# A GRU scan on one core: both rows of x on ScalarE's DMA queue, and r's first products two chunks at a time

## The chip, the cores and the metric

The kernel runs on one core of a Trainium2 chip. The metric is device time in microseconds of one execution, median over runs; lower is better. A profiled execution gives a span as well, from the first to the last instruction of the program, which is a little shorter than the time. Engines are named as in the profile: PE (TensorE), with PEld for its weight loads, DVE (VectorE), ACT (ScalarE), POOL (GpSimd) and SP (SyncE); ACTq, SPq and POOLq are the DMA-issuing sides of those engines.

## The reference

A GRU runs over 128 steps of x (64 batch rows, 128 steps, 512 features), and its states are added to x. After every fourth step but the last the state goes through one more layer.

```python
def step(h, inp):
    x_t, prop = inp
    comb = jnp.concatenate([x_t, h], axis=-1)
    z = jax.nn.sigmoid(comb @ Wz + bz)
    r = jax.nn.sigmoid(comb @ Wr + br)
    comb2 = jnp.concatenate([x_t, r * h], axis=-1)
    h_cand = jnp.tanh(comb2 @ Wh + bh)
    h_new = (1.0 - z) * h + z * h_cand
    h_next = jnp.where(prop, jnp.tanh(h_new @ Wp + bp), h_new)
    return (h_next, h_new)
_, ys = jax.lax.scan(step, h0, (xs, do_prop))
# returned: x + transpose(ys)
```

Wz, Wr and Wh are 1024 x 512; their upper half multiplies x, their lower half h (or r * h). Everything is float32.

## The kernel before

**Tiling.** The batch of 64 is split into two halves of 32 rows (S = 2, V = 32), and the 512 output features into four blocks of 128. A product is written as several matmuls of 128 x 32 weights against 256 columns, each of which fills a block of 32 partitions of a PSUM bank; four of them stand side by side. K = 4 counts the chunks of 128 features over which a product is summed. In the trace each float32 matmul shows as two records.

**Products with x.** The parts of the gates that depend on x alone are made ahead of the recurrence. For step 0 and step 1 they are plain products: `plain(t, (i,))` gives for gate i (0 is r, 1 is z, 2 is the candidate) four units, one for each chunk k, and `now` runs units for both halves at once. Later steps take them in groups of four steps with a Strassen-like scheme (`batch`, `batches`), whose operands POOL and DVE sum up. They fill the gaps between the recurrent products (`fill`).

**Order.** The schedule is manual: the instructions of each engine run in the order in which the program emits them. An engine that waits holds all that stands behind it on that engine.

**The start**, around which the change lies:

- Lines 137 to 141: two rows of x, steps 0 and 1, each 64 x 512 float32 (128 KB), go into `x_rows`, step 0's over SP's queue and step 1's over ACT's (`both_queues`).
- Lines 142 and 143: `load_wx(R, k0, k1)` loads the upper half of Wr in three pieces over SP's queue: chunk 0 (256 KB), chunk 1 (256 KB), and chunks 2 and 3 (512 KB). z's and the candidate's upper halves follow in two pieces each (line 151), then step 2 of x in four (`load_step`, line 122), and further on the lower halves, `wh`.
- Line 145: the biases come over POOL's queue. Line 147: a sigmoid on one element makes ACT load its table early.
- Line 154: a copy of one element of `wx` on POOL waits for r's third piece; behind it POOL issues the loads of h0 (line 156).
- `idle(n)` (line 236) runs n matmuls on zeros (128 x 32 against 512 columns of bf16). `idle(28)` is the first thing on PE.
- `turn_rows(0, ...)` and `turn_rows(1, ...)` (line 306) transpose the rows of step 0 and step 1 on PE, four transposes each, and DVE copies the result into `xT` (line 311). All eight transposes stand on PE ahead of r's first product.
- `split_bias` (lines 205 to 210) is work of DVE. Then come four more fillers, and r's products: chunk 0 of step 0, chunk 0 of step 1, chunk 1 of step 0, chunk 1 of step 1, and then chunks 2 and 3 of the one and of the other. Step 0's go to bank `scratch_q`, step 1's to `scratch_a`; line 246 is the matmul of all products.
- Then follow z's first chunks (`scratch_r`, `scratch_x`), the biases spread over the partitions (line 217), z's other chunks, the candidate's (`scratch_y`), the first eight units of step 2, and the recurrence (`half`).

SP's DMAs each signal one of eight semaphores in rotation; from the ninth DMA on, an issue waits for the landing of the one eight places before it.

Of the kernel before, what the change touches and what calls it, by code (L numbers as in the profile page):

```python
# [18 lines left out]
def kernel(  # L19
# [14 lines left out]
    nc = tc.nc  # L34
    B, T, D = x.shape
# [7 lines left out]
    K = D // P  # L43
# [52 lines left out]
    def part(q):  # L96
        return slice(q * V, (q + 1) * V)
# [15 lines left out]
    both_queues = (nc.sync, nc.scalar)  # L113
# [12 lines left out]
    def load_wx(i, k0, k1):  # L126
# [10 lines left out]
    x_rows = one.tile([P, Q4, S, J], F32, tag="xs0", name="x_rows")[:B].rearrange(  # L137
        "b t h u -> b (t h u)"
    )
    for t in range(2):  # L140
        both_queues[t].dma_start(out=x_rows[:, ts(t, D)], in_=x[:, t, :])  # L141
    for k0, k1 in ((0, 1), (1, 2), (2, K)):
        load_wx(R, k0, k1)
    for i, b in enumerate((br, bh, bz)):
# [10 lines left out]
    for h in range(S):  # L155
        nc.gpsimd.dma_start(
            out=h_rows[:, h, :],
            in_=h0[ts(h, V), :].rearrange("b (q j) -> q b j", q=NQ),
# [44 lines left out]
    def split_bias():  # L203
        high, low = thirds[:NQ], thirds[2 * V : 2 * V + NQ]
        nc.vector.tensor_copy(high, bias_in)
        nc.vector.tensor_sub(rest, bias_in, high)
        nc.vector.tensor_copy(middle, rest)
        nc.vector.tensor_copy(thirds[V : V + NQ], middle)
        nc.vector.tensor_sub(rest, rest, middle)
        nc.vector.tensor_copy(low, rest)  # L210
# [23 lines left out]
    def idle(n):  # L234
        for i in range(n):
            nc.tensor.matmul(
                rec[i // NQ % 3].rearrange("p a d n -> p (a d n)")[part(i % NQ)],
                lhsT=zeros[:, :V],
                rhs=zeros,
                start=True,  # L240
                stop=True,
            )
# [441 lines left out]
    def now(units):  # L684
        put(units)
        both(len(units))
# [3 lines left out]
    turn_rows(0, scratch[4])  # L690
    turn_rows(1, scratch[3])
    split_bias()
    idle(4)
    for part_k in (slice(0, 1), slice(1, 2), slice(2, K)):
        for t in range(2):
            now(first[R][t][part_k])
    load_wh(R)
# [373 lines left out]
```

## Time and profile before

| | us |
|---|---|
| time, median of 3 runs | 1259.13 (1259.06 to 1259.54) |
| time of the profiled execution | 1258.66 |
| its span | 1256.6 |

The mean granted clock of TensorE was 1.000 over the span.

How to read the lines that follow in the prediction. A row of a timeline has the start and the length in us of a group of equal instructions, engine, line, operation, what it writes and reads, shapes and count, and in brackets the idle time of the engine before it and what released it. A row of stretches has the stretch, its length, then for PE, PEld, DVE, ACT and POOL the busy time with the number of instructions, and at last the granted clock of TensorE, the busy share of the 16 DMA engines and the GB/s that they moved. A row of the chain has start, length and place. A row of waits has the waiting engine and line, the releaser, the total in us, the number of waits and the longest. A row of DMA issues has what was moved, the issuing queue, the count, the KB of one, and the median us from issue to landing. Matmuls are pipelined and their ends are modelled, so the spacing of their starts says more than their lengths.

### The profile page before, as it was taken

Reading aid. Unit: us, or ns where it says so; the run is one execution under the profiler, and the core shown is the slowest. Engines: PE = TensorE matmul, PEld = TensorE weight load, DVE = VectorE, ACT = ScalarE, POOL = GpSimd, SP = SyncE. Lnnn points to the kernel's source line nnn. Section 1 sums busy time; section 2 is a strip of 40 time slices with the busy share of each in tenths; the row PEclk is TensorE's granted clock in tenths of the full one; section 3 lists DMA queues with packets and bytes.
Section 4 is the critical chain, followed back from the end, with each engine's and each line's share of the span. In section 5 each row is a group of like instructions: output and inputs, shape, how many; then the busy total and the mean of one; then the engine's idle time right before and its main releaser. Section 6 shows DMA issues by size and latency. Waiting matters only on the chain.

```text
span 1256.6 us, 60732 instructions
## 1 busy us (share of the span) xinstructions
PE 1248.4 (99%) x25952; PEld 1155.6 (92%) x25952; DVE 809.1 (64%) x2183; ACT 836.3 (67%) x2687; POOL 909.7 (72%) x1032
## 2 busy tenths in 40 slices
PE   9999999999999999999999999999999999999998
PEld 5899999999999999999999999999999999999975
DVE  5666666666666666666666666666666666666554
ACT  2566666666666676666666666666676666666665
POOL 4988777777876788767777677787777787677530
PEclk9999999999999999999999999999999999999999
DMA  7311212121122120121111211111211112111011
GB/s 244 96 32 43 52 36 53 39 52 41 32 53 50 40 52 22 51 54 37 53 30 44 52 47 43 41 46 39 53 37 49 40 37 54 45 45 36 13 37 25
DMA packets 112290, 61.09 MB, mean 49 GB/s; under 512 B 12777, under 2 KB 109301, under 8 KB 112021
## 3 DMA queue, kind: packets, MB, share of 16 engines
q1 hardware_dynamic: 111588, 56.90, 17.0%
q8 instruction: 205, 3.36, 1.2%
q14 instruction: 65, 0.52, 0.1%
q0 software_dynamic: 256, 0.14, 0.1%
q10 hardware_dynamic: 176, 0.16, 0.1%
HBM read 40.38 MB, written 16.78 MB: 45 GB/s over the span
## 4 chain that ended last, share of the span: by engine, by line
PE 98%; DMA 1%; issue 1%; SPq 0%; DVE 0%; POOLq 0%; POOL 0%; ACT 0%; ACTq 0%
PE rec L246 45%; PE rec_z L246 16%; PE scratch_r L246 14%; PE scratch_q L246 11%; PE scratch_a L246 5%; PE scratch_y L246 4%; PE scratch_x L246 4%; DMA wx<-in_L_cond_Wr_dram 0%; SPq L886 0%; DMA out_dram<-xr 0%; SPq L127 0%; POOLq L1066 0%; POOL xr L876 0%; DVE z L980 0%; SPq L141 0%
## 5 line engine op out<-in xcount | busy, mean ns | idle before, releaser
L246 PE MATMUL rec<-wh,rhT 128*32 128x256 f32 x4096 | 376.6, 379 | 0.0
L246 PE MATMUL rec<-wh,hT 128*32 128x256 f32 x3072 | 282.9, 379 | 0.0
L246 PE MATMUL rec_z<-wh,hT 128*32 128x256 f32 x3072 | 282.8, 379 | 0.0
L246 PEld LDWEIGHTS rec<-wh,rhT 128*32 128x32 f32 x4096 | 248.5, 110 | 22.3 <-ACT rec L442 1.2
L281 ACT ACTIVATE scratch_r<-rec 64x128 f32<-64x128 f32 x512 | 128.0, 250 | 132.9 <-PE rec L246 65.3
L442 ACT COPY rec<-cp 64x256 f32<-64x256 f32 x512 | 189.9, 371 | 20.2 <-DVE cp L483 0.3
L246 PEld LDWEIGHTS rec<-wh,hT 128*32 128x32 f32 x3072 | 186.7, 110 | 16.2 <-issue 1.9
L246 PEld LDWEIGHTS rec_z<-wh,hT 128*32 128x32 f32 x3072 | 193.3, 110 | 8.1
L281 ACT ACTIVATE rec_z<-rec_z 64x128 f32<-64x128 f32 x488 | 122.0, 250 | 91.1 <-PE rec_z L246 79.2
L281 ACT ACTIVATE c<-rec 64x128 f32<-64x128 f32 x512 | 138.8, 271 | 60.7 <-PE rec L246 48.8
L876 POOL TENSOR_TENSOR xr<-xr,h 128x256 f32<-128x256 f32 x125 | 109.4, 876 | 85.3 <-DVE h L993 83.0
L621 POOL TENSOR_TENSOR cp<-mb,mb 128x768 f32<-128x768 f32 x76 | 139.2, 1831 | 9.3 <-DVE mb L587 5.7
L621 POOL TENSOR_TENSOR mb<-mb,mb 128x768 f32<-128x768 f32 x58 | 106.3, 1833 | 45.5 <-DVE mb L587 45.5
L621 POOL TENSOR_TENSOR cp<-mb 128x768 f32<-128x768 f32 x46 | 84.3, 1832 | 56.9 <-ACT rec_z L442 55.5
L246 PE MATMUL scratch_r<-tw,s 128*32 128x192 f32 x928 | 120.8, 326 | 0.0
L560 ACT COPY cq<-scratch_q 128x384 f32<-128x384 f32 x212 | 102.0, 481 | 19.2 <-PE scratch_q L246 17.7
L577 DVE TENSOR_TENSOR cx<-scratch_r,cx 128x384 f32<-128x384 f32 x106 | 59.1, 557 | 84.1 <-PE scratch_r L246 68.8
L246 PE MATMUL scratch_q<-tt,s 128*32 128x192 f32 x928 | 103.5, 326 | 0.0
L941 DVE SCALAR_TENSOR_TENSOR keep<-rec_z,h 128x256 f32<-128x256 f32 x91 | 38.6, 425 | 94.8 <-ACT rec_z L281 87.4
L583 DVE TENSOR_TENSOR mb<-scratch_q,cx 128x384 f32<-128x384 f32 x106 | 59.1, 558 | 62.4 <-ACT cq L560 62.4
L918 DVE TENSOR_TENSOR rh<-scratch_r,h 128x128 f32<-128x128 f32 x192 | 56.0, 292 | 61.2 <-ACT scratch_r L281 61.2
L246 PE MATMUL rec<-wp,hT 128*32 128x256 f32 x992 | 91.6, 379 | 0.1
(207 smaller groups left out, 3851.0 us busy)
## 6 DMA issues: line engine op xcount, KB each, us to landing
out_dram<-xr SPq DMA_DIRECT2D x249, 64.0 KB, 1.8
xr<-in_x_dram SPq DMA_DIRECT2D x248, 64.0 KB, 2.3
xs<-in_x_dram SPq DMA_DIRECT2D x240, 64.0 KB, 2.1
wx<-in_L_cond_Wz_dram SPq DMA_DIRECT2D x2, 512.0 KB, 7.8
wx<-in_L_cond_Wh_dram SPq DMA_DIRECT2D x2, 512.0 KB, 9.1
wh<-in_L_cond_Wr_dram SPq DMA_DIRECT2D x2, 512.0 KB, 7.7
wh<-in_L_cond_Wz_dram SPq DMA_DIRECT2D x2, 512.0 KB, 5.7
wh<-in_L_cond_Wh_dram SPq DMA_DIRECT2D x2, 512.0 KB, 9.4
```

The source lines that it names most:

```text
L246: nc.tensor.matmul(ps[part(2 * h + c)], lhsT=left, rhs=rhs(c), start=start, stop=True, skip_group_check=True,)
L281: nc.scalar.activation(o, v, func)
L442: nc.scalar.copy(gate_ps(i, h)[rows].rearrange("p d (c n) -> p d c n", c=C), G[t][rows, :, :, i, :].rearrange("p c d n -> p d c n"),)
L560: nc.scalar.copy(c[:, :nm], ps[:, :nm])
L577: nc.vector.tensor_add(T2[what][:, :nm], r_ps[:, :nm], T2[what][:, :nm])
L583: nc.vector.tensor_add(blocks(1, 1), runs(q_ps[:, :nm]), runs(T2[what][:, :nm]))
L621: nc.gpsimd.tensor_add(dst, a, b)
L876: nc.gpsimd.tensor_add(o, o, h_new.rearrange("p h (k e) -> p h e k", k=K))
L918: nc.vector.tensor_mul(rh[:, h, :], r_, h_old[:, h, :])
L941: nc.vector.scalar_tensor_tensor(out=kept[0], in0=kept[1], scalar=1.0, in1=kept[2], op0=ALU.subtract, op1=ALU.mult,)
```

## The change

Both rows of x are issued on ScalarE's queue, step 0's first. SyncE's queue so begins with r's weights, whose three pieces stay as they are. On PE two fillers instead of four stand behind the transposes, and r's products of chunks 0 and 1 run for step 0 and then for step 1, where before the steps alternated chunk by chunk. Chunks 2 and 3 run as before. Nothing else on any engine changes its place.

```diff
     for t in range(2):
-        both_queues[t].dma_start(out=x_rows[:, ts(t, D)], in_=x[:, t, :])
+        nc.scalar.dma_start(out=x_rows[:, ts(t, D)], in_=x[:, t, :])
     for k0, k1 in ((0, 1), (1, 2), (2, K)):
         load_wx(R, k0, k1)
...
     turn_rows(0, scratch[4])
     turn_rows(1, scratch[3])
     split_bias()
-    idle(4)
-    for part_k in (slice(0, 1), slice(1, 2), slice(2, K)):
+    idle(2)
+    for part_k in (slice(0, 2), slice(2, K)):
         for t in range(2):
             now(first[R][t][part_k])
     load_wh(R)
```

## The prediction

> **What bounds the kernel now.** I read the page first, its busy shares and its chain; then a table of three stretches; then, inside the first of them, the chain in order of time.
>
> ```profile
> span 1256.6 us, 60732 instructions
> PE 1248.4 (99%) x25952; PEld 1155.6 (92%) x25952; DVE 809.1 (64%) x2183; ACT 836.3 (67%) x2687; POOL 909.7 (72%) x1032
> PE 98%; DMA 1%; issue 1%; SPq 0%; DVE 0%; POOLq 0%; POOL 0%; ACT 0%; ACTq 0%
> 0.00:14.00 14.00, 11.73 (x176) 6.28 (x180) 7.75 (x22) 2.41 (x5) 3.97 (x12) 1.00 0.81 264
> 14.00:1240.00 1226.00, 1225.93 (x25608) 1141.49 (x25604) 794.54 (x2139) 826.08 (x2655) 904.84 (x1019) 1.00 0.18 46
> ```
>
> In the two rows of stretches the first column after the length is the busy time of PE: from 14 to 1240 us it is busy for 1225.93 of 1226.00 us. Nothing that this change touches lies there, and no instruction of that stretch changes. So the edit can move only the moment at which PE becomes continuous, and everything behind it slides by the same amount. That moment is in the first 14 us, where 14.00 - 11.73 = 2.27 us of PE are idle.
>
> ```profile
> 0.75 0.62 SPq L141
> 1.43 0.80 SPq L127
> 2.27 0.52 SPq L127
> 2.84 6.12 DMA wx<-in_L_cond_Wr_dram
> 9.01 1.07 PE scratch_q L246 x16
> 10.08 0.86 PE scratch_a L246 x16
> 10.94 0.86 PE scratch_r L246 x16
> 11.81 0.86 PE scratch_x L246 x16
> PE rec L236 <- DVE zeros L67: 1.2, 1, 1.2
> PE scratch_q L246 <- DMA wx<-in_L_cond_Wr_dram: 1.1, 1, 1.1
> ```
>
> The chain (start, length, what) says what the start hangs on: SP issues x's row of step 0, then r's three weight loads (256, 256 and 512 KB), and PE goes continuous at 9.01 when the third has landed at 8.96. The waits of PE put 1.1 us on that load. The other idle time is the 1.2 us before the first filler, which stays. Call the three loads c0, c1 and c2.
>
> **The change part by part.** First the queue. Removing the x issue from SP's head takes 1.43 - 0.75 = 0.68 us from in front of c0, c1, c2 and all that SP issues behind them. With the same lengths c0 is issued at 0.75, c1 at 1.59, c2 at 2.12 us.
>
> ```profile
> wx<-in_L_cond_Wr_dram SPq DMA_DIRECT2D x2, 256.0 KB, 4.3
> wx<-in_L_cond_Wr_dram SPq DMA_DIRECT2D x1, 512.0 KB, 6.1
> x_rows<-in_x_dram SPq DMA_DIRECT2D x1, 128.0 KB, 3.3
> x_rows<-in_x_dram ACTq DMA_DIRECT2D x1, 128.0 KB, 2.8
> 2.00:3.00 1.00, 1.00 (x16) 0.43 (x12) 0.22 (x1) 0.85 (x2) 1.00 (x3) 1.00 0.84 242
> 3.00:4.00 1.00, 1.00 (x16) 0.20 (x8) 0.00 (x0) 0.00 (x0) 0.21 (x1) 1.00 0.51 123
> 4.00:5.00 1.00, 1.00 (x10) 0.70 (x6) 0.00 (x0) 0.00 (x0) 0.00 (x0) 1.00 0.82 256
> 5.00:6.00 1.00, 1.00 (x13) 0.57 (x15) 0.85 (x2) 0.00 (x0) 0.00 (x0) 1.00 0.92 309
> 8.00:9.00 1.00, 0.00 (x0) 0.00 (x0) 0.95 (x3) 0.00 (x0) 0.00 (x0) 1.00 1.00 326
> ```
>
> The last number of the issue rows is the time from issue to landing; the last two of the stretches are the busy share of the 16 DMA engines and GB/s. If c2 keeps its 6.1 us, it lands 0.68 us earlier, at 8.28: one bound. The other bound is no shift: the bytes in front of c2's end are the same 2 x 128 + 2 x 256 + 512 KB, and from 5 us on the engines are 0.92 to 1.00 busy, so an earlier issue only helps if the engines have idle time to fill. They have: 0.51 busy from 3 to 4 us and 0.82 from 4 to 5, which is 0.49 + 0.18 = 0.67 us, just while c0 is not flowing yet. I take 0.6 of 0.68, near the upper bound because that hole is as large as the shift; c2 lands near 8.36.
>
> Second, the row of step 1 now goes behind that of step 0 on ScalarE's queue.
>
> ```profile
> 0.76 0.58 ACTq L141 DMA_DIRECT2D x_rows<-in_x_dram  x1
> 1.37 1.28 ACT L147 ACT_TABLE_LOAD   x1 [1.37 <-PEq L1057]
> 12.93 0.65 ACT L226 COPY bias_x<-scratch_y 128x256 f32<-128x256 f32 x2 [10.07 <-PE scratch_y L217]
> 3.73 0.64 PE L236 MATMUL rec<-zeros 128*32 128x512 bf16 x4
> 4.30 0.74 PE L306 MATMUL scratch_y<-ident,x_rows 64*128 64x64 f32 x4
> 4.84 0.68 PE L306 MATMUL scratch_x<-ident,x_rows 64*128 64x64 f32 x4
> 5.45 0.62 PE L236 MATMUL rec<-zeros 128*32 128x512 bf16 x4
> 5.91 0.73 PE L246 MATMUL scratch_q<-wx,xT 128*32 128x256 f32 x8
> 6.45 0.62 PE L246 MATMUL scratch_a<-wx,xT 128*32 128x256 f32 x8
> 6.88 0.62 PE L246 MATMUL scratch_q<-wx,xT 128*32 128x256 f32 x8
> 7.32 0.62 PE L246 MATMUL scratch_a<-wx,xT 128*32 128x256 f32 x8
> 5.56 0.42 DVE L311 COPY xT<-scratch_x 128x256 f32<-128x256 f32 x1
> ```
>
> ScalarE's table load and the dummy sigmoid behind it move by the 0.58 us of an issue; the next work there is at 12.93 after 10.07 us idle, so this costs nothing (without that cover, 0.58). Step 0's row lands at 0.76 + 2.8 = 3.6 us (was 0.75 + 3.3 = 4.05); the fillers run to about 3.73 + 0.43 (their spacing) = 4.16, so its transposes start near 4.2 instead of 4.30. Step 1's row is issued at 0.76 + 0.58 = 1.34 and lands at 1.34 + 2.8 = 4.1 at best; at worst it takes c0's 4.3 us beside c0 and lands at 5.6. Its transposes ran at 4.84. They stand in PE's own order, so a late row holds them, the two fillers and r's products behind them: 0 to 0.8 us. Does that reach the path? In the worst case the transposes run to 6.2, the fillers to 6.7, and the four groups of eight records (0.43 apart, 1.8 us in all) to 8.5: 0.1 behind c2. Nearest to the rows of the x loads themselves is 4.1 to 4.7, which costs nothing; I take nothing, with 0.2 as the far end.
>
> Third, the order of the first two chunks. The same 32 records run, first 16 of step 0, then 16 of step 1. Step 0's second chunk needs c1, now at about 1.59 + 4.3 = 5.9, and its first needs the fillers' end; so they run from about 5.9 to 7.7, as before (5.91 to 7.75). Step 1's copy on DVE, done at 5.98, is not wanted before 6.8; a copy up to 0.8 late is free. The gain of this reordering is slack, no time: behind it PE waits for c2 anyway, then from 7.7 to 8.36.
>
> Fourth, two fillers fewer. Four of them took 5.45 to 5.91; they run side by side, so two save between 0 and half of that, 0.23 us. All of it lies ahead of the wait for c2: worth 0, and without that cover 0.23 at most.
>
> What is late next when c2 comes at 8.36?
>
> ```profile
> 10.49 0.43 DVE L362 TENSOR_TENSOR tt<-wx 128x256 f32<-128x256 f32 x1 [1.30 <-DMA wx<-in_L_cond_Wz_dram]
> 16.61 0.67 DVE L297 STREAM_TRANSPOSE xT<-xr 128x256 f32<-128x256 f32 x1 [1.13 <-DMA xr<-in_x_dram]
> 18.00 3.64 PE L246 MATMUL scratch_q<-wx,xT 128*32 128x256 f32 x64
> ```
>
> z's first weights released DVE at 10.49 and PE used them at 10.76 (9.01 + 2 x 0.87): 0.3 us of slack, and as the loads behind c2 stand in the same queue they move with it. If they moved only half as far (0.3), they would come at 10.2, just when PE is there. (SP's later issues wait in turn for the landing of earlier loads, and in that rotation x's two rows stay first and second.) Step 2's transpose ends at 17.28, and the 64 records that read it start at 18.00: 0.72 us of slack even if its load did not move at all. So the 0.6 us passes through.
>
> The sum, against the profiled execution: 8.96 - 8.36 = 0.6 gained, 0 for the rest, so its 1258.66 us become 1258.06. That execution (span 1256.6 and 2.1 around it) lies 0.47 under the median of the runs, 1259.13; for the median I predict 1258.5 us.
>
> The Trainium skill, page "DMA: Bandwidth & Descriptors", section "Issuing engines are not separate DMA queues", says that issuing from several engines saves only sequencer time and that all transfers share the same 16 DMA engines. By it the sum keeps the 0.68 us of issuing as its ceiling, and if the shared engines were the whole limit it would be rival B's 1259.1; the 0.51 of the third microsecond speaks for the first.
>
> **The rivals.**
>
> A, the forecast above: 1258.5, chance 0.45.
>
> B, **the transfer is no earlier**: c2 ends with its slowest DMA engine, and if that engine has no hole from 3 to 5 us, its same bytes end at 8.9. For: the engines as a whole go from 0.92 to 1.00 until 9 us, and c2 needs 6.1 us for 512 KB where the mean rate of 309 GB/s would carry it and c1 in 2.5. Against: the hole. Gain 0 to 0.2, 1259.0; chance 0.18.
>
> C, **PE's slow start lasts longer**, the slower one. The first eight of r's records take 6.45 - 5.91 = 0.54 us and the next 0.43: until about 6.2, five us after the first filler at 1.20, PE ran slower, the fillers too. How much slower is bounded by the granted clock of an idle PE at the end:
>
> ```profile
> 1256.00:1256.60 0.60, 0.00 (x0) 0.00 (x0) 0.00 (x0) 0.00 (x0) 0.00 (x0) 0.50 0.06 14
> ```
>
> that is, half. If the wait for step 1's row (0 to 0.8 us, at 4.7) makes PE count its five us again, full pace comes at 10 or later. The 32 records then run at 0.86 a group from 6.0 to 9.5, the third chunk's first 0.5 us at half pace, and that chunk ends near 11.4 instead of 10.76: 0.65 lost, 1259.8. It decides from 8.7 us on: with full pace at 8.7, products from 5.9 would end at 5.9 + 3.46 + 1.4 = 10.76. Against: step 1's row probably lands in time, and a wait of 1.07 us ahead of 9.01 left the groups behind it at 0.43. Chance 0.14.
>
> The Trainium skill, page "TensorE: Matmul & The Clock Gate", section "Part 1: The HAM clock gate (the "warmup" mystery)", has the clock at half until about 3.4 us of sustained activity. By that figure, an estimate from the page, one missed window puts full pace at 6.2 + 3.4 = 9.6 and the time at about 1259.6.
>
> D, **the wait for c2 vanishes**: c2 comes by 7.7, when PE is done with the first chunks. Then z's first weights are next: 10.49 - 0.68 = 9.8 instead of 10.76, a gain of 1.0, of which the 0.72 of slack at 18.00 passes for certain. 1258.1 to 1258.4. For: c2's 6.1 us is long for its bytes. Against: nothing makes the engines faster. Chance 0.15.
>
> E, something outside the first 14 us: the 98% of PE would have to change by 0.2%, and no row offers a cause. Chance 0.08, either sign.
>
> **How the numbers follow.** A change under 0.2%, 2.5 us, is about what a measurement of this kernel can't tell from none. A to D all lie within it (their ends are 1.0 faster and 1.4 slower), so same has 0.92, and E is split 0.03 faster and 0.05 slower, more to the slower side because C could last longer than worked out. The range takes in D with 0.3 of the runs' scatter (1258.1 - 0.3) and C's middle: 1257.8 to 1259.9; left out are E and the worst of C, some 0.15. A alone would be 1258.2 to 1258.9.
>
> **What would show it.** In the trace after: SP's first issue is r's weights at 0.75; the DMA share from 3 to 4 us is over 0.8; PE's record at 9.01 stands at 8.3 to 8.5 with a wait for c2 of 0.5 to 0.9 before it; step 1's transposes start by 4.9; the groups of eight are 0.43 apart from the second on; the row of 14 to 1240 is as full as now. A start of the third chunk at 8.9 is B, groups 0.86 apart past 8.7 is C, no wait for c2 is D. A difference over 2.5 us would make the whole argument wrong.

## The result, and the profile after

The changed kernel is slower: 1261.60 us (median of 19 runs, 1260.79 to 1262.32) against 1259.13 us for the kernel before (19 runs, 1257.47 to 1261.46), a ratio of 1.0019 with a 95% interval of 1.0012 to 1.0027. The forecast was 1258.5 with a range up to 1259.9; the time lies outside it, on the side of rival C. The profiled execution took 1261.57 us.

The page after, and the two stretches that were read before:

```profile
span 1259.5 us, 60728 instructions
PE 1249.9 (99%) x25950; PEld 1170.0 (93%) x25950; DVE 808.6 (64%) x2183; ACT 836.4 (66%) x2687; POOL 908.4 (72%) x1032
0.00:14.00 14.00, 10.40 (x110) 5.39 (x113) 6.45 (x19) 1.49 (x2) 3.92 (x12) 1.00 0.89 268
14.00:1240.00 1226.00, 1225.94 (x25620) 1154.53 (x25616) 793.69 (x2137) 825.76 (x2654) 902.75 (x1018) 1.00 0.17 46
```

From 14 us on PE is as full as before (1225.94 of 1226.00). The loss is in the first 14 us, and there PE is busy for less time (10.40 against 11.73) and gets fewer instructions done (110 against 176). The chain in order of time has a new first link:

```profile
0.75 0.55 ACTq L141
...
1.33 6.11 DMA x_rows<-in_x_dram
7.49 0.74 PE scratch_x L306 x4
8.23 0.54 PE rec L236 x2
8.78 1.71 PE scratch_q L246 x16
10.48 1.71 PE scratch_a L246 x16
12.19 0.90 PE scratch_q L246 x16
```

Step 1's row of x needs 6.11 us on ScalarE's queue and sets the start; r's third piece has left the chain. The timeline of PE and its waits:

```profile
5.83 0.71 PE L306 MATMUL scratch_y<-ident,x_rows 64*128 64x64 f32 x4 [1.46 <-DMA x_rows<-in_x_dram]
7.49 0.74 PE L306 MATMUL scratch_x<-ident,x_rows 64*128 64x64 f32 x4 [0.94 <-DMA x_rows<-in_x_dram]
...
8.18 2.30 PE L246 MATMUL scratch_q<-wx,xT 128*32 128x256 f32 x16
9.89 2.30 PE L246 MATMUL scratch_a<-wx,xT 128*32 128x256 f32 x16
11.60 1.49 PE L246 MATMUL scratch_q<-wx,xT 128*32 128x256 f32 x16
12.72 1.22 PE L246 MATMUL scratch_a<-wx,xT 128*32 128x256 f32 x16
13.59 1.22 PE L246 MATMUL scratch_r<-wx,xT 128*32 128x256 f32 x16
```

Two things are to be seen. The transposes wait for both rows, 1.46 and 0.94 us. And then sixteen records take 9.89 - 8.18 = 1.71 us, where eight took 0.43 before: PE runs at half pace until about 12.1, and sixteen take 0.86 only from 12.72 on. By starts of groups, from step 1's transposes to z's first product (`scratch_r`): the transposes are 7.49 - 4.84 = 2.65 later; from them to the first product 0.69 instead of 1.07, -0.38; the first 32 records 3.42 instead of 1.84, +1.58; the wait for r's third piece, from 7.75 to 9.01, is gone, -1.26; the third chunk 1.99 instead of 1.75, +0.24. Together 2.83, which is 13.59 - 10.76; the span grew by 2.9.

The landings and the stretch from 4 to 6 us, of the changed kernel:

```profile
wx<-in_L_cond_Wr_dram SPq DMA_DIRECT2D x2, 256.0 KB, 4.7
wx<-in_L_cond_Wr_dram SPq DMA_DIRECT2D x1, 512.0 KB, 6.8
tw<-in_L_cond_br_dram POOLq DMA_DIRECT2D x1, 2.0 KB, 6.1
DMA to landing us min/median/max: 4.9/5.5/6.1
8.53 0.17 POOL L154 COPY held<-wx 1x1 f32<-1x1 f32 x1 [5.31 <-DMA wx<-in_L_cond_Wr_dram]
4.00:6.00 2.00, 0.55 (x6) 0.20 (x2) 0.00 (x0) 0.00 (x0) 0.00 (x0) 1.00 1.05 221
```

and the same stretch, and one bias, of the kernel before:

```profile
4.00:6.00 2.00, 2.00 (x20) 1.27 (x20) 0.85 (x2) 0.00 (x0) 0.00 (x0) 1.00 0.87 283
tw<-in_L_cond_br_dram POOLq DMA_DIRECT2D x1, 2.0 KB, 3.2
```

The fourth line is the view of `x_rows`: the rows took 4.9 and 6.1 us, where they took 2.8 and 3.3. r's third piece releases POOL's copy at 8.53 instead of 9.02: 0.49 us earlier between these two executions, though it took 6.8 us from its issue instead of 6.1. The engines are busier from 4 to 6 us (1.05 against 0.87) and move less (221 against 283 GB/s).

### The profile page after: what moved, and what is told of

It is laid out like the page before. It is cut to its first block, busy times and chain, and to the rows that moved or that the text cites. A ratio compares the mean times of both kernels' runs of the same rounds, so it can differ in the third digit from the quotient of the medians.

```text
span 1259.5 us, 60728 instructions
## 1 busy us (share of the span) xinstructions
PE 1249.9 (99%) x25950; PEld 1170.0 (93%) x25950; DVE 808.6 (64%) x2183; ACT 836.4 (66%) x2687; POOL 908.4 (72%) x1032
## 4 chain that ended last, share of the span: by engine, by line
PE 98%; DMA 1%; issue 1%; DVE 0%; SPq 0%; POOLq 0%; POOL 0%; ACTq 0%; ACT 0%
PE rec L246 44%; PE rec_z L246 16%; PE scratch_r L246 14%; PE scratch_q L246 11%; PE scratch_a L246 5%; PE scratch_y L246 4%; PE scratch_x L246 4%; DMA x_rows<-in_x_dram 0%; SPq L886 0%; DMA out_dram<-xr 0%; POOLq L1066 0%; POOL xr L876 0%; PE scratch_x L306 0%; DVE z L980 0%; DVE xr L983 0%
```

## The experiments

Theory T: the rows of x, sharing the DMA engines with r's weights from the start, land late; PE pauses, and its slow start lasts into r's products. Rival O: PE's own order (fewer fillers, two chunks at once) does it. The times of the kernel before, in brackets, were measured together with each run. The start of z's first product in each profile is a second measure: span less this start is 1245.6 to 1246.0 us in all twelve kernels, so differences between profiled executions arise ahead of it, but for 0.4 us. The last column is the moment, from the span's start, at which the trace's record of the granted clock begins, with full clock; it holds nothing earlier, and only the spacing of PE's records shows the half pace before it.

| kernel | median us (before) | ratio, 95% | z's first product at | span | full clock from |
|---|---|---|---|---|---|
| before | 1259.13 | | 10.76 | 1256.6 | 6.15 |
| changed | 1261.60 (1259.13) | 1.0019, 1.0012 to 1.0027 | 13.59 | 1259.5 | 12.13 |
| queues alone | 1261.78 (1258.57) | 1.0025, 1.0015 to 1.0035 | 14.07 | 1259.9 | 12.90 |
| PE's order alone | 1258.87 (1258.57) | 1.0002, 0.9993 to 1.0011 | 11.29 | 1256.9 | 9.73 |
| changed, waits filled | 1259.53 (1258.57) | 1.0006, 0.9998 to 1.0015 | 11.52 | 1257.4 | 6.53 |
| both rows on SyncE | 1258.54 (1258.57) | 1.0002, 0.9993 to 1.001 | 10.40 | 1256.2 | 4.10 |
| one DMA on ScalarE | 1261.22 (1258.78) | 1.0021, 1.0011 to 1.003 | 14.15 | 1260.1 | 13.37 |
| big first piece | 1262.69 (1258.78), one run | | 14.74 | 1260.6 | 13.07 |
| r's first piece on ScalarE | 1259.13 (1258.78) | 1.0002, 0.9993 to 1.0011 | 11.46 | 1257.3 | 9.68 |
| short fill | 1259.33 (1258.78) | 1.0006, 0.9997 to 1.0015 | 11.23 | 1256.9 | 9.83 |
| one DMA on SyncE | 1259.41 (1259.03) | 1.0003, 0.9995 to 1.0012 | 11.30 | 1257.0 | 4.84 |
| first wait filled | 1259.51 (1259.03) | 1.001, 1.0 to 1.0019 | 11.23 | 1257.1 | 4.97 |

**Queues alone.**

```diff
-        both_queues[t].dma_start(out=x_rows[:, ts(t, D)], in_=x[:, t, :])
+        nc.scalar.dma_start(out=x_rows[:, ts(t, D)], in_=x[:, t, :])
```

> The edit to the queues alone: both rows of x on ScalarE's queue, PE's fillers and order as before. Theory T: the whole loss comes from the rows of x, which now share the DMA engines with r's first weights from the start and land late (about 5.7 and 7.4 us after the start of the span, as in the changed kernel); PE then waits and starts r's products near 8.5 at half pace. It expects the changed kernel's time, 1261.5 +- 0.7 us. Rival O (PE's order: two fillers fewer, two chunks of a step at once) expects the time of the kernel before, 1259.1 +- 0.7.

It carries the whole loss and somewhat more (1261.78, +3.2 us). Its timeline of PE:

```profile
7.30 0.74 PE L306 MATMUL scratch_x<-ident,x_rows 64*128 64x64 f32 x4 [0.89 <-DMA x_rows<-in_x_dram]
7.97 0.62 PE L236 MATMUL rec<-zeros 128*32 128x512 bf16 x4
8.37 1.07 PE L246 MATMUL scratch_q<-wx,xT 128*32 128x256 f32 x8
9.23 1.07 PE L246 MATMUL scratch_a<-wx,xT 128*32 128x256 f32 x8
```

The same late row, and eight records in 0.86 us, with four fillers and the old order. O falls.

**PE's order alone.**

```diff
-    idle(4)
-    for part_k in (slice(0, 1), slice(1, 2), slice(2, K)):
+    idle(2)
+    for part_k in (slice(0, 2), slice(2, K)):
```

> The edit to PE alone: two fillers and two chunks of a step at once, x's rows on SyncE's and ScalarE's queues as before. T expects the rows to land at 4.1 and 3.6 us, the third chunk's products to start with the landing of r's third piece near 9.0 and 1259.1 +- 0.7 us. O expects a loss of 1.5 us or more against the kernel before: 1260.6 or later.

1258.87, not to be told from the kernel before, as T expected. But the profile holds a surprise. Its timeline of PE:

```profile
6.00 1.93 PE L246 MATMUL scratch_q<-wx,xT 128*32 128x256 f32 x16
7.68 1.96 PE L246 MATMUL scratch_a<-wx,xT 128*32 128x256 f32 x16
9.39 1.23 PE L246 MATMUL scratch_q<-wx,xT 128*32 128x256 f32 x16
```

Here too PE ran at half pace until past 9.39, with no wait. It cost little, because the records ended near the moment at which r's third piece released PE in the kernel before (9.01). Half pace is cheap until r's third piece is there. And the time of full pace is not fixed by the program alone: in the kernel before, in this one and in the one with both rows on SyncE PE runs the same fillers at the same times, without a break, up to 4.2 us, and yet the clock turned full at 6.15, 9.73 and 4.10. A theory of late rows alone would be too simple: the pace had to be tested by itself.

**The waits filled.**

```diff
-    idle(28)
+    idle(44)
     turn_rows(0, scratch[4])
+    idle(12)
     turn_rows(1, scratch[3])
```

> The changed kernel with 16 more fillers ahead of the transposes of step 0 and 12 between those of step 0 and step 1, so that PE is busy while it waits for x. T splits the loss of the changed kernel (third chunk starting at 12.19 instead of 9.01) into the late row and the half pace of r's first 32 records (3.42 us instead of 1.9). If the half pace comes from PE idling in the waits, the groups of eight are 0.43 us apart from their start, the third chunk starts near 10.5 and the time is about 1260.0 (1.6 less than the changed kernel). If idling is not what keeps the pace low, the groups stay 0.86 apart and the time is 1261.6 or, as the fillers may run over, up to 1 us more.

1259.53 us, in eleven runs from 1259.42 to 1259.68, all below the lowest of the changed kernel (1260.79). Against the kernel before, measured with each, the loss falls from 2.47 us to 0.96. The timeline of PE:

```profile
7.40 0.69 PE L306 MATMUL scratch_x<-ident,x_rows 64*128 64x64 f32 x4
8.02 0.39 PE L236 MATMUL rec<-zeros 128*32 128x512 bf16 x2
8.04 1.24 PE L246 MATMUL scratch_q<-wx,xT 128*32 128x256 f32 x16
8.93 1.21 PE L246 MATMUL scratch_a<-wx,xT 128*32 128x256 f32 x16
9.79 1.21 PE L246 MATMUL scratch_q<-wx,xT 128*32 128x256 f32 x16
```

The second row of x is as late as in the changed kernel (7.40 against 7.49), but sixteen records take 0.86 us, and z's product comes at 11.52 instead of 13.59. Of these 2.07 us between the two profiles, 1.67 lie in the first 32 records (1.75 instead of 3.42), 0.26 in the third chunk (1.73 instead of 1.99), which the expectation had left out, and 0.14 ahead of both. So of the 2.83 us that the changed kernel's profile is later than that of the kernel before, 1.93 are half pace, and 0.90 the late row.

**The first wait filled**: the changed kernel with more fillers in one place.

```diff
-    idle(28)
+    idle(44)
     turn_rows(0, scratch[4])
```

> The changed kernel with 16 more fillers ahead of step 0's transposes only; PE still pauses about 0.9 us between the two sets of transposes. The half pace comes from PE's pauses before about 7.4 us. If the length of the pauses together (2.4 us) is what matters, filling the first 1.5 brings full pace as in the run with both filled (6.5), groups of 0.43 and 1259.5. If any pause of 0.9 us ahead of the products is enough, the groups stay at 0.86 until past 10 us and the time is 1261.0 or more.

Neither expectation alone: six runs took 1259.29 to 1259.51 and five 1260.74 to 1261.41, nothing between. The profiled one (1259.32) is of the first group, with z's product at 11.23 and this on PE:

```profile
5.00 0.60 PE L236 MATMUL rec<-zeros 128*32 128x512 bf16 x8
...
7.12 0.69 PE L306 MATMUL scratch_x<-ident,x_rows 64*128 64x64 f32 x4 [0.90 <-DMA x_rows<-in_x_dram]
7.74 0.39 PE L236 MATMUL rec<-zeros 128*32 128x512 bf16 x2
7.76 1.24 PE L246 MATMUL scratch_q<-wx,xT 128*32 128x256 f32 x16
8.64 1.21 PE L246 MATMUL scratch_a<-wx,xT 128*32 128x256 f32 x16
```

A pause of 0.90 us between the transposes did not slow PE there. But the clock had turned full ahead of it, at 4.97: the eight fillers from 5.00 take 0.53 us, where eight took 0.86 before. So what a pause of 0.9 us does to a PE still at half pace this profile doesn't show. That the second group of runs is the one at half pace is argued from its distance of 1.2 to 2.1 us; no profile shows it. Its five runs have a mean granted clock of 0.998 each, the other six 0.999 each. That mean sees only the return to half pace at the end of the program, so it says that the clock changed at other moments in the two groups, and not which of them began at half pace.

**Short fill**, half pace with early rows, in the kernel before:

```diff
-    idle(28)
+    idle(12)
```

> The kernel before with 12 instead of 28 fillers at the start: PE pauses from about 2.5 us until step 0's row lands near 4.1; queues as before. It prices the half pace by itself, with the rows early. If a pause of PE ahead of the products keeps it at half pace, the groups of eight are 0.86 us apart for r's first 32 records (5.9 to 9.4), and full pace comes near 9.7 or later; with r's third piece at 9.0 that costs 0.4 to 1.5 us: 1259.0 to 1260.1. If the pause doesn't matter, groups of 0.43 and 1258.6.

```profile
4.24 0.71 PE L306 MATMUL scratch_y<-ident,x_rows 64*128 64x64 f32 x4 [1.57 <-DMA x_rows<-in_x_dram]
...
6.61 1.11 PE L246 MATMUL scratch_a<-wx,xT 128*32 128x256 f32 x8
7.46 1.11 PE L246 MATMUL scratch_q<-wx,xT 128*32 128x256 f32 x8
```

These rows of PE show the pause and eight records in 0.85 us; the clock turned full at 9.83. PE's order alone had nearly the same without a pause (9.73), so this one profile doesn't show that the pause did it. It prices the half pace with the rows early: z's product comes at 11.23, 0.47 later than before; the median is 0.55 higher, with an interval that still holds no change, and the runs scatter from 1258.08 to 1261.8.

**Both rows on SyncE's queue**, r's weights behind them; PE as changed.

```diff
-        nc.scalar.dma_start(out=x_rows[:, ts(t, D)], in_=x[:, t, :])
+        nc.sync.dma_start(out=x_rows[:, ts(t, D)], in_=x[:, t, :])
```

> The changed kernel's PE order, but both rows of x at the head of SyncE's queue, ahead of r's weights, nothing on ScalarE's queue. T (what matters is that r's weights do not flow beside the rows) expects the rows to land by 4.1 and 4.9 us, r's weights to be issued 0.6 us later than before and its third piece to land near 9.5: 1259.7 +- 0.7 us. A rival, that two rows one behind the other on one queue are slow in themselves, expects the second row at 6 us or later and 1261 or more.

Landings, and PE:

```profile
x_rows<-in_x_dram SPq DMA_DIRECT2D x2, 128.0 KB, 2.8
wx<-in_L_cond_Wr_dram SPq DMA_DIRECT2D x1, 512.0 KB, 5.1
8.24 1.07 PE L246 MATMUL scratch_q<-wx,xT 128*32 128x256 f32 x16 [0.15 <-DMA wx<-in_L_cond_Wr_dram]
10.40 1.07 PE L246 MATMUL scratch_r<-wx,xT 128*32 128x256 f32 x16 [0.22 <-DMA wx<-in_L_cond_Wz_dram]
```

Two rows behind one another are not slow in themselves: a median of 2.8 us. Nor is ScalarE's queue, which carried step 1's row in 2.8 us in the kernel before. What is left is the weights that flow beside them. PE starts on r's third piece at 8.24, though it was issued at 3.13, 0.29 us after that of the kernel before (2.84); the time is level with it (1258.54 against 1258.57). The third piece varies: with the queues of before it took 6.1 us in the first profile, and these in the profiles of PE's order alone and of the short fill:

```profile
wx<-in_L_cond_Wr_dram SPq DMA_DIRECT2D x1, 512.0 KB, 5.5
```

```profile
wx<-in_L_cond_Wr_dram SPq DMA_DIRECT2D x1, 512.0 KB, 5.3
```

**How the two queues share**: in turns of whole issues (Q), or evenly by packets (S). First both rows in one DMA on ScalarE's queue, then r's first two pieces as one load.

```diff
-    for t in range(2):
-        nc.scalar.dma_start(out=x_rows[:, ts(t, D)], in_=x[:, t, :])
+    nc.scalar.dma_start(out=x_rows[:, : 2 * D].rearrange("b (t u) -> b t u", t=2), in_=x[:, :2, :])
```

> The changed kernel with both rows of x in one DMA on ScalarE's queue (64 runs of 4 KB, 256 KB). Theory Q: transfers of the two queues are begun in turn, a whole issue at a time (r's first piece, step 0's row, r's second piece, step 1's row, r's third). It expects both rows behind r's first piece alone, landed by about 6.2 us where step 1's row took until 7.44: step 1's transposes start near 6.5 instead of 7.49 and the time is 1.0 us or more below the changed kernel, 1260.5. Rival S: the two queues share the engines evenly packet by packet, so that bytes on the ScalarE side land at half the rate however they are cut: both rows by 7.4 as before, step 0's transposes later, 1261.5.

```profile
x_rows<-in_x_dram ACTq DMA_DIRECT2D x1, 256.0 KB, 5.9
6.83 0.71 PE L305 MATMUL scratch_y<-ident,x_rows 64*128 64x64 f32 x4 [2.46 <-DMA x_rows<-in_x_dram]
7.34 0.68 PE L305 MATMUL scratch_x<-ident,x_rows 64*128 64x64 f32 x4
```

Both rows land by 0.75 + 5.9 = 6.7, between the two expectations. The time did not follow Q: step 0's transposes now start only at 6.83, step 1's only 0.15 earlier than in the changed kernel, and the half pace stays (1261.22).

```diff
-    for k0, k1 in ((0, 1), (1, 2), (2, K)):
+    for k0, k1 in ((0, 2), (2, K)):
```

> The changed kernel with r's first two pieces as one load of 512 KB at SyncE's head. Read for the landings only. Q (turns of whole issues) expects step 0's row behind 512 KB instead of 256, landing 0.7 to 0.9 us later than in the changed kernel (5.69), near 6.5, and step 1's row behind r's third piece, near 8.5 or later. S (even sharing by packets) expects both rows where they were, 5.7 and 7.4, or earlier.

```profile
6.57 0.71 PE L306 MATMUL scratch_y<-ident,x_rows 64*128 64x64 f32 x4 [2.19 <-DMA x_rows<-in_x_dram]
8.84 0.74 PE L306 MATMUL scratch_x<-ident,x_rows 64*128 64x64 f32 x4 [1.56 <-DMA x_rows<-in_x_dram]
```

A larger piece of r ahead pushes step 0's row back by 0.7 (5.83 to 6.57 at the transposes) and step 1's by 1.35 (7.49 to 8.84). Q expected just this. The trace shows a turn, too: between 5.2 and 6.1 us ScalarE's queue moved no packet and SyncE's 116, though step 1's row had been issued at 1.3; even sharing by packets leaves no such gap. Turns by issue fit the landings of both runs, one profile each, better than even sharing; which unit makes the turns is not shown.

**Two tries at a better version.** r's first piece behind step 1's row on ScalarE's queue, in the kernel before:

```diff
-    for k0, k1 in ((0, 1), (1, 2), (2, K)):
-        load_wx(R, k0, k1)
+    load_wx(R, 0, 1, nc.scalar)
+    load_wx(R, 1, 2)
+    load_wx(R, 2, K)
```

> The kernel before with r's first piece moved to ScalarE's queue, behind step 1's row: the rows of x stay at the head of both queues, and r's second and third piece and all behind them are issued about 0.8 us earlier on SyncE's queue. PE as before. T (weights are welcome early as long as the rows go first) expects the rows at 3.6 to 4.2 us as before, r's third piece to land 0.3 to 0.8 us earlier than 8.96, and 1258.3 us, 0.2 to 0.7 below the kernel before. A rival, that a piece of r on ScalarE's queue is as late as x was there, expects r's first piece at 7 us or later, and a loss of 0 to 1 us.

A miss. Step 0's row slowed to a landing of 4.0 us (3.3 before), r's third piece took 7.1 (6.1), and the time is level, 1259.13 against 1258.78. Then both rows in one DMA at SyncE's head, r's weights behind, PE as changed:

```diff
-        nc.scalar.dma_start(out=x_rows[:, ts(t, D)], in_=x[:, t, :])
+    nc.sync.dma_start(out=x_rows[:, : 2 * D].rearrange("b (t u) -> b t u", t=2), in_=x[:, :2, :])
```

> A version meant to beat both: PE as in the changed kernel, and both rows of x in one DMA of 256 KB at the head of SyncE's queue, r's weights behind it at the same issue times as in the kernel before (the second issue on SyncE's queue saved). The theory (rows first, then weights, one turn for the rows) expects both rows by about 4.4 us, r's third piece at 8.2 to 8.9, z's first piece by 10.0 and 1258.2 us, 0.3 to 0.6 below the kernel before. If the stream of weights is no faster than when the rows went over two queues, it is the time of the kernel before.

Also a miss: the rows took 4.0 us, r's pieces 4.8 and 7.0, and the time is level, 1259.41 against 1259.03. No version faster than the kernel before was found.

## Why the prediction was wrong, by its own steps

**What bounds the kernel** held: nothing past the first 14 us changed, and the loss is the shift of PE's continuous start.

**First, the queue**: not borne out. r's third piece was issued at 1.67 and not at 2.12, as the three issues took 1.35 us together instead of 1.84, and the DMA engines were 0.91 busy from 3 to 4 us, as forecast. It was to land at 8.36 and did by 8.53, 0.49 ahead of the profile before. But it took 6.8 us, and in the two other profiles with the old queues (PE's order alone, short fill) it released POOL's copy at 8.34 and 8.06. So no gain of the earlier issue is shown, and the 8.96 on which the term rested was a late one.

**Second, the row of step 1**: this step failed. Its landing was bounded by 5.6, from 1.34 plus c0's own 4.3 us "beside c0", and 0 was taken, with 0.2 at the far end. The bound priced the row with a landing that had been measured almost alone: c0 landed at 1.43 + 4.3 = 5.7, and the row on ScalarE's queue had landed at 3.6. Measured: 6.11 us from 1.33, landing at 7.44; step 0's row, put at 3.6, came at 0.75 + 4.9 = 5.7. The edit puts weights beside the rows, and both streams took longer (r's pieces 4.7 and 6.8 us, where they took 4.3 to 4.4 and 5.3 to 6.1). The prediction counted the fuller DMA engines as a pure gain, though the rows were what had to pass first. So the term taken at 0 measured 2.83 us between the profiles: 0.90 of the late row, and 1.93 of the half pace behind it, which rival C had apart.

**Third and fourth**, the order and the fillers: right to be counted as nothing; alone they measure 1.0002 (0.9993 to 1.0011).

**Rival C** had the mechanism, the sign and the place, with a chance of 0.14 and a price of 0.65. The loss was 2.83, for two reasons: the row was 2.65 late and not up to 0.8, and the half pace lasted until about 12.1. Its point of decision, full pace later than 8.7, was passed. Its assumed count of five us from the end of the pause does not hold as a fixed one. Seven profiles have a pause for x while PE is at half pace. In six of them full clock comes 4.2 to 6.5 us after the end of the last pause (changed 4.6, queues alone 5.6, one DMA on ScalarE 6.5, big first piece 4.2, r's first piece on ScalarE 4.8, short fill 5.6). In the seventh, one DMA on SyncE, it comes at 4.84, just as a pause of 0.47 us ends. The pause of 0.90 us in the run with the first wait filled came at full pace and did not end it.

The traces give a figure as well. From the moment in the table's last column to the return to half pace near the end, the clock is full for 1249.28 us in five profiles and for 1245.87 in seven, 366 and 365 times 3.413. That fits a clock that can change only every 3.41 us, at moments that fall differently in each execution; it is an inference from these lengths.

The page "TensorE: Matmul & The Clock Gate" of the Trainium skill, in its Part 1, ties full speed to sustained activity of about 3.4 us. The run with filled waits agrees in kind: a PE kept busy through the same waits had groups of eight at 0.43, and one that paused at 0.86. The step of 3.41 us agrees with the figure. But activity of that length did not suffice in the run of PE's order alone: PE was busy from 1.20 without a wait, and the clock turned full only at 9.73. Why is not shown.

**B and D**: whether the third piece gained, B's question, is left open by its scatter. PE didn't wait for it, as D has it, but only because PE itself came late. E had 0.05 for slower by more than 0.2%; the ratio of 1.0019 stays just inside that bound, though its interval reaches to 1.0027, and the loss lies inside the first 14 us.

## What to carry to other kernels

A load that the first work waits for is priced with what will flow beside it, not with its duration in the old trace: with other transfers on a second queue from the same moment, step 1's row landed after 6.1 us instead of 2.8. Before a wait is moved or lengthened at the start, ask whether PE will still be at full pace behind it; filling the waits with idle matmuls gave back 2.07 of 2.83 us between the profiles here, and 1.5 of 2.5 by the medians. Weights that come earlier are worth nothing until the operand that meets them is there.

## What was not expected of the hardware

Small transfers suffer with the large ones: the 2 KB of br's bias took 6.1 us to land instead of 3.2. From 4 to 6 us the DMA engines, with two streams, were fully busy (1.05) and moved 221 GB/s; with one they moved 283 at 0.87. Why packets take longer then stays open.

The granted clock in the rows of stretches reads 1.00 even where PE runs at half pace. In the changed kernel:

```profile
8.00:10.00 2.00, 2.00 (x22) 1.10 (x25) 1.13 (x3) 0.00 (x0) 1.47 (x3) 1.00 1.06 409
```

The column ahead of the last two says 1.00, while the timeline gives 1.71 us for sixteen records. The trace's record of the clock begins only at 12.13 us there, and what is ahead of it counts as full; so does the mean of 1.000 that the kernel before shows. At the start of a program the pace is read from the spacing of equal instructions.

The moment of full pace varies between executions whose PE has done the same up to 4.2 us: 4.10, 6.15 and 9.73 us, as said above. The times fit that: of the kernel with the first wait filled five runs of eleven took 1.2 to 2.1 us longer than the rest, and none lay between; and of the changed kernel the seven runs with a mean granted clock of 0.998 took 1260.79 to 1261.27 us, the twelve with 0.999 or 1.000 took 1261.46 to 1262.32. This suggests that part of the scatter of a kernel's times is where the clock's changes fall; it is not shown run by run.
